# Fused RWKV, soft tree, attention and expert layers on one core: group-long runs of value matmuls, two head groups in one PSUM bank, single full-width transposes

## The chip, the cores and the metric

The kernel runs on one core of a Trainium2 chip. The time is the device time of one execution in microseconds (us). A core has a matrix engine (PE), which multiplies a stationary block of up to 128x128 by a moving block and adds into PSUM, and three other compute engines: VectorE (DVE), ScalarE (ACT) and GpSimd (POOL). PSUM has eight banks of 128 partitions by 512 floats. SyncE (SP) issues every DMA of this kernel, in one queue, in order. Each engine executes its own instructions in the order of the program and waits at an instruction until what it needs is there.

## The reference, cut to what matters

The input is 16 sequences of 512 positions with 128 features. Four sublayers follow one another, each followed by a layer normalisation of input plus output: an RWKV block (time mixing with two scans over the positions, then channel mixing), a soft decision tree of depth 8, causal attention, and a mixture of 16 experts of which two count at each position. The change touches the attention and the experts:

```python
scores = jnp.einsum('bthd,bshd->bhts', q, k) / jnp.sqrt(jnp.float32(dh))   # 16 heads of 8
scores = scores + causal[None, None, :, :]
weights = jax.nn.softmax(scores, axis=-1)
out = jnp.einsum('bhts,bshd->bthd', weights, v).reshape(b, seq, d)
...
topk_vals, topk_idx = jax.lax.top_k(s, TOP_K)
g_topk = jnp.sum(jax.nn.one_hot(topk_idx, N_r) * topk_vals[..., None], axis=-2)
routed = jnp.einsum('bse,bseo->bso', g_topk, xe)
```

## The kernel before

One sequence b is one batch of work; its 512 positions are four tiles of 128 (`NT`). The 16 heads are taken in four groups of four (`NG`, `HG`). Float32 operands of the queries and keys are split into three bfloat16 parts each, so that one bfloat16 matmul with 72 rows gives a score; three more rows of the query operand (`qo[QK_ROWS...]`) carry the negated row maximum, again in three parts, against a constant in the key operand.

For every batch and group of heads, these pieces follow one another:

- `operands` (line 833) loads the query and key operands of a group by DMA into one of three sets.
- `greatest` (line 854) computes the scores `sc` with queries on the partitions, adds the causal mask by one more matmul (stationary `identb`, moving `masks`, line 869), and DVE takes the maximum (line 871). POOL splits the 16 maxima of each partition into three bfloat16 parts (`nm3`, lines 876 to 881). PE turns the parts by four transposes of 128x12 into a bank `pmx`, one for each tile of positions (line 885), ACT copies 12x512 to `rows` (line 888), and three DMAs put the three parts into the query operand (line 891).
- `weighted` (line 910) computes the scores again with keys on the partitions, now with the maximum subtracted (`st`, line 927; mask at line 929), and ACT writes the exponentials into a tile `ew` of 128x4x512, one for each of the four key tiles kt. There are two such tiles (`e_slots`).
- `sums` (line 940) multiplies the exponentials by the values. The stationary operand has 32 columns: eight values of a head, a column of ones that gives the sum of the weights, and columns that are not used. Each of the four heads j writes its own 32 partitions of bank `o`, so a key tile is four float32 matmuls that run side by side (line 950). A key tile's four matmuls stand in PE's order as soon as its exponentials are due, so other PE work may lie between key tiles.
- `ends` (line 956) copies `o` to SBUF (`os`), turns it by four transposes (`pot`, line 969), and DVE divides by the sums (`rec`, `att`). After four groups come the output projection, the residual and the normalisation to `u`.
- `gating` (line 1007) finds the two greatest gates of each position, writes them into `gaug` (four tiles of 16 columns), turns them by four transposes (`pg`, line 1057), copies 16x512 to `gT` and sends it to DRAM with one DMA (line 1066), from where the gates are spread to all partitions (line 1080). `by_gate` multiplies `u` by each gate on POOL, `experts` sums the 16 experts in bank `acc`.

Ahead of these, `front` (line 570) computes the RWKV block and the tree of a batch.

All these pieces are Python generators that a planner (`Plan`, line 69) interleaves while the program is built: it keeps an estimated clock for each engine, with estimated costs (`tensor_us` and its like), and emits the instruction whose due time comes first, where the due time is the moment it became ready plus a slack by piece and engine (`S_FRONT` to `S_EXPERTS`). `PERIOD` and `LEAD` say when a batch's `front` may begin, `SCORES` how many banks may hold scores at a time. The planner fixes each engine's order; on the chip nothing is reordered by it. It sees the DMAs only as fixed delays, for instance 3.0 us for the rows of maxima.

Of the kernel before, what the change touches and what calls it, by code (L numbers as in the profile page):

```python
# [39 lines left out]

HAND_OVER = 0.2
BANKS = 8
SCORES = 5
PERIOD = 96.0

S_FRONT = {"PE": -6.0, "V": -6.0, "A": 0.0, "G": 0.0}
S_RWKV = {"PE": -10.0, "V": 3.0, "A": -30.0, "G": 3.0}
S_GREATEST = {"PE": -30.0, "V": 0.0, "A": -3.0, "G": 0.0}
S_WEIGHTED = {"PE": -15.0, "A": 3.0, "G": -10.0}
S_SUMS = {"PE": 10.0}  # L50
S_ENDS = {"PE": 6.0, "V": -3.0, "A": 0.0, "G": -15.0}
S_GATE = {"PE": 6.0, "V": 6.0, "A": 6.0, "G": 30.0}
S_EXPERTS = {"PE": 30.0}
FREE = {}
LEAD = 60.0
RWKV_PACE = 8.0
HOLD = 16
HOLD2 = 0
SPLIT = 2
EXPERT_PACE = 1.0  # L60
# [186 lines left out]
def tensor_us(op, out, w, x, *_):  # L247
    n = columns(out)
    if out.shape[0] == 32:
        return 0.02 + 0.0005 * n  # L250
    if x.dtype == BF16:
        return 0.02 + 0.0004 * n
    return 0.01 + 0.0009 * n if op == "transpose" else max(0.2, 0.0018 * n)
# [11 lines left out]
def pool_us(op, out, *_):  # L265
    return 0.25 + 0.0022 * columns(out)
# [3 lines left out]
def rwkv_tree_attn_moe(ctx: ExitStack, tc: tile.TileContext, a: dict, out: bass.AP):  # L270
# [30 lines left out]
    e_slots, us_slots, gb_slots = Slots(plan, 2), Slots(plan, 3), Slots(plan, 2)  # L301
# [28 lines left out]
    w_at = load("w_at", pool=p2, tag="e4")  # L330
# [108 lines left out]
    masks, idents = (fixed(x, [128, HG, 128], BF16) for x in ("masks", "idents"))  # L439
    mask, identb = masks[:, 0, :], idents[:, 0, :]  # L440
    w_qkv, w_o = fixed("w_qkv", [128, 3, D]), fixed("w_o", [128, D])

    vaug = fixed("vaug", [128, NT, NH * (DH + 1) + 23])
    vheads = vaug[:, :, 0:NH * (DH + 1)].rearrange("p t (h c) -> p t h c", c=DH + 1)
    qops, kops = ([fixed(f"{x}{i}", [128, HG, T], BF16) for i in range(OPERANDS)] for x in ("qop", "kop"))
    zeros = dram.tile([PARTS, HG, T], BF16, tag="zeros", name="zeros")

    def prepare_attention():

        G.memset(vaug, 1.0)  # L450
        for i in range(OPERANDS):
            for op, x in ((qops[i], 0.0), (kops[i], TWO_ONES)):
                V.memset(op.rearrange("p h t -> p (h t)").bitcast(F32), x)
            if i == 0:
                nc.sync.dma_start(out=zeros, in_=qops[i][0:PARTS])
            yield
# [4 lines left out]
        for i in range(HG):  # L461
            copy(masks[:, i, :], mask32)
            copy(idents[:, i, :], ident)
# [3 lines left out]
        for i in range(2):  # L467
            V.tensor_scalar(w_qkv[:, i, :].rearrange("p (d h) -> p d h", h=NH),
                            w_at[:, 2 * i * D:(2 * i + 1) * D].rearrange("p (h d) -> p d h", d=DH), col(V_NORM), None, ALU.mult)
            yield  # L470
# [8 lines left out]
    gaugs = [fixed(f"gaug{i}", [128, NT, NE]) for i in range(2)]  # L479
# [374 lines left out]
    def greatest():  # L854

        for b in range(B):
            for g in range(NG):
# [3 lines left out]
                for t in range(NT):  # L861
                    w = (t + 1) * 128
                    per = min(HG, 512 // w)
                    for h in range(0, HG, per):
# [4 lines left out]
                        mm(sc[:, :, t * 128:w], identb, masks[:, 0:per, :], start=False, stop=True)  # L869
# [6 lines left out]
                nm3 = p2.tile([128, NT, PARTS, HG], BF16, tag="nm3", name="nm3")  # L876
                yield
                G.tensor_copy(nm3[:, :, 0, :], nmx)
                G.tensor_tensor(nmx, nmx, nm3[:, :, 0, :], ALU.subtract)
                G.tensor_copy(nm3[:, :, 1, :], nmx)  # L880
                G.tensor_tensor(nm3[:, :, 2, :], nmx, nm3[:, :, 1, :], ALU.subtract)
                yield
                pt = yield from bank("pmx", (128, 512), BF16)
                for t in range(NT):
                    tr(pt[0:PARTS * HG, t * 128:(t + 1) * 128], nm3[:, t].rearrange("p a h -> p (a h)"), identb)
                yield
                rows = p2.tile([PARTS * HG, T], BF16, tag="rows", name="rows")
                copy(rows, pt[0:PARTS * HG, :])
                give(pt)
                for i in range(PARTS):  # L890
                    nc.sync.dma_start(out=qo[QK_ROWS + i:QK_ROWS + i + 1, :, :], in_=rows[HG * i:HG * (i + 1), :])
# [7 lines left out]
    def values(b, keep):  # L899
        if b:  # L900
            yield event("o", b - 1, NG - 1)
# [4 lines left out]
        copy(vheads[:, :, :, 0:DH], pv.rearrange("p (t h d) -> p t h d", t=NT, d=DH))  # L906
# [3 lines left out]
    def weighted():  # L910

        for b in range(B):
            for g in range(NG):
# [4 lines left out]
                for kt in range(NT):  # L918
                    slot_e = yield e_slots
                    n_q = T - kt * 128  # L920
                    per = min(HG, 512 // n_q)
                    e = p2.tile([128, HG, T], F32, tag="e4", name="ew")
                    for h in range(0, HG, per):
                        slot = yield scores
                        sc = yield from bank("st", (128, per, n_q))
                        for i in range(per):
                            mm(sc[:, i, :], ko[:, h + i, kt * 128:(kt + 1) * 128], qo[:, h + i, kt * 128:T],
                               start=(i == 0), stop=False)
                        mm(sc[:, :, 0:128], mask, idents[:, 0:per, :], start=False, stop=True)
                        yield  # L930
                        act(e[:, h:h + per, 0:n_q], sc, AF.Exp)
# [4 lines left out]
                    kept["e", b, g, kt] = e, slot_e  # L936
                    event("e", b, g, kt).set()
                sets.put(n)

    def sums():  # L940
        for b in range(B):
            yield event("values", b)
            for g in range(NG):
                for kt in range(NT):
                    yield event("e", b, g, kt)
                    e, slot_e = kept.pop(("e", b, g, kt))
                    if kt == 0:
                        o = yield from bank("o")
# [254 lines left out]
```

## Time and profile before

| What | Value |
|---|---|
| time of three runs | 1764.74, 1766.97 and 1767.44 us; median 1766.97 |
| span of the profiled execution, first to last instruction | 1762.0 us |
| granted PE clock, mean over the span | 0.970 |
| PE busy | 1623.4 us, 92% |
| DVE, ACT and POOL busy | 1270.0, 1172.3 and 1014.9 us |
| DMA | 133.78 MB, 24% of 16 engines' span |

The profile gives the span of its execution and no other time of it; the three times are those of runs of the same program, and their median is 5.0 us above the span.

Nearly all instructions are issued by one helper, so they carry one line number (L231), and groups are told apart by the names of their tiles: `o<-ew,vaug` is the matmul that writes bank `o` from the exponentials and the values. A float32 matmul appears as two records (x2 for one). "128*32" ahead of the shape is the part of the array that the stationary operand fills: 128 rows by 32 columns. In the timeline, the first number is the start in us from the span's beginning. Matmuls overlap: the duration of a record is the time from its start until its last result, while the time that it takes from PE is the distance from its start to the start of the next.

### The profile page before, as it was taken

How to read it: one execution, taken by the hardware profiler on the slowest of the kernel's cores; microseconds unless marked ns; L12 is line 12 of the kernel's file. 1: busy time of each engine (PE TensorE's matmuls, PEld its weight loads, DVE VectorE, ACT ScalarE, POOL GpSimd, SP SyncE). 2: the span in 40 equal slices, each digit the busy share in tenths (PEclk: the TensorE clock that was granted, in tenths of full speed). 3: DMA queues.
4: the chain of work that ended last, by engine and by line, in shares of the span. 5: the costliest groups of instructions: out<-in, count | busy, mean ns of one | idle time of the engine just before them, and what ended most of it. 6: DMA issues, size and time to landing. Idle time of an engine off the chain costs nothing.

```text
span 1762.0 us, 25378 instructions
## 1 busy us (share of the span) xinstructions
PE 1623.4 (92%) x8604; PEld 770.6 (44%) x8604; DVE 1270.0 (72%) x1928; ACT 1172.3 (67%) x1976; POOL 1014.9 (58%) x1321
## 2 busy tenths in 40 slices
PE   4567889899999999999999999999999999998976
PEld 1233334344444444454454444444444444454532
DVE  6686879687876869687776868687776868653633
ACT  3345677667768677777868677776768686675531
POOL 1345545557484756758474767757575746746323
PEclk8788999999999999999999999999999999999998
DMA  3001011212213232312222232312313122324323
GB/s 108 0 7 59 21 33 35 95 47 93 76 65 96 75 106 65 90 58 82 88 77 89 82 96 75 112 59 76 93 53 120 63 80 69 101 77 117 103 76 122
DMA packets 61970, 133.78 MB, mean 76 GB/s; under 512 B 11708, under 2 KB 32974, under 8 KB 61585
## 3 DMA queue, kind: packets, MB, share of 16 engines
q1 hardware_dynamic: 61841, 132.16, 24.1%
q8 instruction: 69, 1.13, 0.3%
q14 instruction: 60, 0.49, 0.1%
HBM read 114.01 MB, written 17.31 MB: 75 GB/s over the span
## 4 chain that ended last, share of the span: by engine, by line
PE 63%; DVE 11%; POOL 9%; ACT 6%; DMA 6%; issue 3%; SPq 1%; POOLq 0%; DVEq 0%; ACTq 0%
PE acc L231 9%; PE st L231 8%; PE sc L231 8%; PE p L231 7%; PE o L231 7%; PE pv L231 4%; DVE sk L231 4%; PE ph L231 3%; PE pr L231 3%; PE pk L231 2%; POOL us L231 2%; DMA gb<-gd 2%; DVE skv L231 2%; PE pvv L231 2%; POOL four L231 2%
## 5 line engine op out<-in xcount | busy, mean ns | idle before, releaser
L231 DVE TENSOR_REDUCE nmx<-sc 128x1 f32<-128x384 f32 (+3 forms) x704 | 439.0, 636 | 210.7 <-PE sc L231 208.8
L231 ACT ACTIVATE ew<-st 128x512 f32<-128x512 f32 (+1 forms) x704 | 380.8, 556 | 215.7 <-PE st L231 212.0
L231 POOL TENSOR_TENSOR us<-u,gb 128x512 f32<-128x512 f32 x240 | 306.5, 1287 | 186.5 <-PE acc L231 84.0
L231 PE MATMUL acc<-us,w_mo 128*128 128x512 f32 x512 | 268.8, 620 | 13.6 <-POOL us L231 11.5
L231 PE MATMUL st<-qop,kop 128*128 128x512 bf16 (+3 forms) x1024 | 254.5, 303 | 18.2 <-DMA qop<-rows 15.8
L231 PE MATMUL sc<-kop,qop 128*128 128x128 bf16 (+3 forms) x1024 | 256.6, 303 | 0.3
L231 DVE RECIPROCAL sk<-sk 128x512 f32<-128x512 f32 x64 | 213.9, 3343 | 0.0
L231 PE MATMUL o<-ew,vaug 128*32 128x512 f32 (+3 forms) x2048 | 191.5, 447 | 2.5 <-ACT ew L231 2.5
L231 PEld LDWEIGHTS <-qop 128*128 128x128 bf16 x1024 | 93.7, 99 | 183.2 <-issue 163.5
L231 PE MATMUL sc<-masks,idents 128*128 128x128 bf16 (+2 forms) x704 | 172.9, 246 | 0.0
L231 PE MATMUL st<-idents,masks 128*128 128x128 bf16 (+2 forms) x704 | 172.6, 245 | 0.0
L231 PEld LDWEIGHTS <-kop 128*128 128x128 bf16 x1024 | 91.1, 98 | 155.8 <-issue 109.5
L231 POOL TENSOR_TENSOR sk<-fk,sk 128x512 f32<-128x512 f32 x64 | 81.3, 1271 | 103.5 <-DVE sk L231 57.8
L231 POOL TENSOR_TENSOR skv<-t,skv 128x512 f32<-128x512 f32 x64 | 81.3, 1270 | 81.8 <-DVE skv L231 78.7
L231 POOL TENSOR_TENSOR lp<-gates,lp 128x8 f32<-128x8 f32 (+6 forms) x224 | 117.3, 545 | 2.3
L231 PEld LDWEIGHTS acc<-us,w_mo 128*128 128x128 f32 x512 | 83.0, 192 | 73.5 <-issue 39.0
L231 POOL TENSOR_TENSOR rw<-skv,sk 128x512 f32<-128x512 f32 x64 | 86.8, 1356 | 42.8 <-DVE sk L231 41.5
L231 PEld LDWEIGHTS <-idents 128*128 128x128 bf16 x704 | 69.4, 99 | 86.6 <-issue 80.8
L231 PE MATMUL pv<-sq,mean_w 128*128 128x512 f32 x160 | 91.0, 652 | 13.9 <-ACT sq L231 13.8
L231 DVE TENSOR_TENSOR_SCAN sk<-decay,k 128x511 f32<-128x511 f32 x64 | 102.8, 1606 | 0.0
L231 PE MATMUL p<-rw,w_tm 128*128 128x512 f32 x128 | 73.5, 658 | 29.8 <-POOL rw L231 25.6
L231 ACT ACTIVATE r<-pv,eps 128x512 f32<-128x512 f32 x96 | 65.8, 686 | 44.0 <-PE pv L231 25.9
(208 smaller groups left out, 2982.7 us busy)
## 6 DMA issues: line engine op xcount, KB each, us to landing
gb<-gd SPq DMA_DIRECT2D x128, 512.0 KB
qop<-there SPq DMA_DIRECT2D x576, 32.0 KB
kop<-there SPq DMA_DIRECT2D x192, 96.0 KB
there<-parts SPq DMA_DIRECT2D x32, 384.0 KB
x<-xT SPq DMA_DIRECT2D x16, 256.0 KB
out<-sqb SPq DMA_DIRECT2D x16, 256.0 KB
qop<-rows SPq DMA_DIRECT2D x192, 4.0 KB
w_mo<-w_mo SPq DMA_DIRECT2D x1, 1160.0 KB
```

The source lines that it names most:

```text
L231: ins = getattr(self.engine, op)(out, *args, **kw)
```

## The change

- `weighted` computes the key tiles in two pairs, (0, 3) and (1, 2). A pair's exponentials lie side by side in one tile of 128x4x640, of which there are three.
- `sums` waits for both pairs of a group and then issues all sixteen matmuls of the group in one run.
- Two groups share a bank `o`. In the values' layout a head now has 18 columns: nine zeros, eight values, a one. The even group of a pair of groups takes its 32 columns from the values on, the odd one from the zeros on, so their results fall into columns 0 to 8 and 9 to 17 of each head's 32 partitions, and one accumulates on top of the other. `ends` copies and turns a bank once for two groups. The columns of the query and key projections are permuted so that the heads come out in that order.
- The maxima's parts lie 32 columns apart by tile of positions in a fixed tile of 128x128, which one transpose turns; ACT copies 128x128. Four DMAs (one for each tile of positions, three rows by four heads by 128 positions) take the place of three. The gates are laid out, turned and sent likewise, with four DMAs for one.
- The causal mask and the identity are held once and repeated by a zero stride in the operand, not by four copies in memory.
- The planner's constants (slacks, `PERIOD`, `LEAD`, `SCORES`, costs) have other values.

```diff
+E_SLOTS = 3
+PAIRS = ((0, 3), (1, 2))
+HEAD = 2 * (DH + 1)
-SCORES = 5
-PERIOD = 96.0
+SCORES = 7
+PERIOD = 89.5
-S_FRONT = {"PE": -6.0, "V": -6.0, "A": 0.0, "G": 0.0}
...
+S_FRONT = {"PE": -6.0, "V": -21.0, "A": 0.0, "G": 1.0}
+S_RWKV = {"PE": -10.0, "V": 3.0, "A": -6.0, "G": 7.0}
+S_GREATEST = {"PE": -42.0, "V": -3.0, "A": -3.0, "G": 24.0}
+S_WEIGHTED = {"PE": -21.0, "A": 3.0, "G": -22.0}
+S_SUMS = {"PE": 1.0}
...
-LEAD = 60.0
+LEAD = 87.0
...
-                        mm(sc[:, :, t * 128:w], identb, masks[:, 0:per, :], start=False, stop=True)
+                        mm(sc[:, :, t * 128:w], identb, of_heads(mask, per), start=False, stop=True)
...
-                pt = yield from bank("pmx", (128, 512), BF16)
+                pt = yield from bank("pmx", (128, 128), BF16)
+                tr(pt, nm3.rearrange("p t c -> p (t c)"), identb)
+                yield
+                rows = p2.tile([128, 128], BF16, tag="rows", name="rows")
+                copy(rows, pt)
+                give(pt)
                 for t in range(NT):
-                    tr(pt[0:PARTS * HG, t * 128:(t + 1) * 128], nm3[:, t].rearrange("p a h -> p (a h)"), identb)
...
-                for i in range(PARTS):
-                    nc.sync.dma_start(out=qo[QK_ROWS + i:QK_ROWS + i + 1, :, :], in_=rows[HG * i:HG * (i + 1), :])
+                    nc.sync.dma_start(out=qo[QK_ROWS:QK_ROWS + PARTS, :, t * 128:(t + 1) * 128], in_=rows[32 * t:32 * t + PARTS * HG, :])
...
             for g in range(NG):
+                for i in range(2):
+                    yield event("e", b, g, i)
+                if g % 2 == 0:
+                    o = yield from bank("o")
                 for kt in range(NT):
-                    yield event("e", b, g, kt)
-                    e, slot_e = kept.pop(("e", b, g, kt))
-                    if kt == 0:
-                        o = yield from bank("o")
+                    e = kept.pop(("e", b, g, kt))
                     for j in range(HG):
-                        mm(o[32 * j:32 * (j + 1), kt * 128:T], vaug[:, kt, (HG * g + j) * (DH + 1):(HG * g + j) * (DH + 1) + 32], e[:, j, 0:T - kt * 128],
-                           start=(kt == 0), stop=(kt == NT - 1))
-                    e_slots.put(slot_e)
-                kept["o", b, g] = o
-                event("o", b, g).set()
+                        at = HEAD * (8 * (g // 2) + 2 * j + g % 2) + (DH + 1) * (1 - g % 2)
+                        mm(o[32 * j:32 * (j + 1), kt * 128:T], vaug[:, kt, at:at + 32], e[:, j, :],
+                           start=(g % 2 == 0 and kt == 0), stop=(g % 2 == 1 and kt == NT - 1))
+                for i in range(2):
+                    e_slots.put(kept.pop(("slot", b, g, i)))
+                if g % 2:
+                    kept["o", b, g // 2] = o
+                    event("o", b, g // 2).set()
+                yield
...
-            for t in range(NT):
-                tr(pg[0:NE, t * 128:(t + 1) * 128], gaug[:, t, :], ident)
+            tr(pg[:, 0:128], gaug.rearrange("p t c -> p (t c)"), ident)
...
-            nc.sync.dma_start(out=gd, in_=gT)
+            for t in range(NT):
+                nc.sync.dma_start(out=gd[:, t * 128:(t + 1) * 128], in_=gT[32 * t:32 * t + NE, :])
```

## The prediction

> **What bounds the kernel now.** I read the busy shares first, then the slices.
>
> ```profile
> PE 1623.4 (92%) x8604; PEld 770.6 (44%) x8604; DVE 1270.0 (72%) x1928; ACT 1172.3 (67%) x1976; POOL 1014.9 (58%) x1321
> ...
> PE   4567889899999999999999999999999999998976
> ...
> PEclk8788999999999999999999999999999999999998
> ```
>
> PE is at 90% or more in nearly every slice after the first seven, at full clock. Then the stretches of the middle (first number after the bounds: length, second: PE busy, then PEld, DVE, ACT, POOL):
>
> ```profile
> 400.00:600.00 200.00, 196.62 (x1078) 94.35 (x1077) 157.03 (x233) 146.17 (x248) 130.06 (x169) 1.00 0.26 81
> 800.00:1000.00 200.00, 198.73 (x1110) 95.14 (x1103) 154.82 (x231) 150.74 (x253) 129.84 (x163) 1.00 0.26 82
> 1200.00:1400.00 200.00, 197.12 (x1067) 94.25 (x1065) 152.26 (x227) 145.74 (x244) 133.29 (x175) 1.00 0.26 82
> ```
>
> PE is idle 1 to 2% there, the next engine (DVE) is busy 77%. So PE time taken out of this stage comes off the span, as long as PE still finds its inputs ready. A busy PE is not PE at its peak, so I read what each piece takes from start to start in the timeline of PE (start in us, duration, then the operation):
>
> ```profile
> 1270.59 1.02 PE L231 MATMUL pvv<-xv,w_tm 128*128 128x512 f32 x2
> 1271.44 1.02 PE L231 MATMUL p<-rw,w_tm 128*128 128x512 f32 x2
> 1272.39 1.71 PE L231 MATMUL o<-ew,vaug 128*32 128x512 f32 x16
> 1274.04 0.39 PE L231 MATMUL st<-qop,kop 128*128 128x256 bf16 x2
> ...
> 1275.56 1.02 PE L231 MATMUL acc<-us,w_mo 128*128 128x512 f32 x2
> 1276.52 0.39 PE L231 MATMUL pmx<-idents,nm 128*12 128x128 bf16 x4
> 1276.84 0.40 PE L231 MATMUL st<-qop,kop 128*128 128x128 bf16 x4
> 1277.07 0.38 PE L231 MATMUL st<-idents,masks 128*128 128x512 bf16 x1
> 1277.29 0.39 PE L231 MATMUL sc<-kop,qop 128*128 128x128 bf16 x4
> 1277.51 0.38 PE L231 MATMUL sc<-masks,idents 128*128 128x512 bf16 x1
> 1277.82 0.86 PE L231 MATMUL o<-ew,vaug 128*32 128x256 f32 x16
> 1278.61 1.13 PE L231 MATMUL acc<-us,w_mo 128*128 128x512 f32 x2
> 1279.57 0.60 PE L231 MATMUL pot<-ident,os 128*128 128x128 f32 x4
> 1280.01 0.38 PE L231 MATMUL sc<-kop,qop 128*128 128x256 bf16 x2
> ```
>
> The reader sees five prices. A float32 matmul of 512 columns takes 0.85 (1270.59 to 1271.44), but 0.95 when an `o` run follows, and the 512-column mask matmul takes 0.22 (1277.07 to 1277.29), but 0.31 ahead of `o`: entering the 32-column form costs 0.09 to 0.10. The run of 512 and 384 columns takes 1.65; four heads side by side should take 0.85 + 0.64 (384/512 of it) = 1.49, so leaving costs about 0.10 and the staggered starts the rest. In all a run costs 0.19 on top of its columns, whether it holds one key tile or two. A float32 matmul that follows such a run takes 0.96, another 0.10. `pmx` pays the same toll: 0.10 ahead of it, then 0.32 for four transposes. A float32 transpose takes 0.11 (four in 0.44).
>
> **The change part by part, against the span of 1762.0.** Run lengths are counted in the order of the two built programs.
>
> 1. Value matmuls. Before, 210 runs of four and 23 of eight, 233 in all; after, 64 of sixteen. Columns are the same. 169 runs less at 0.19: -32.1.
> 2. Maxima. 64 times 0.10 + 0.32 goes, 64 times 0.056 comes (a 128-column bfloat16 matmul at full width, from the median start-to-start distance of the mask matmuls): -23.3.
> 3. `pot`: 32 banks less to turn, 4 x 0.11 each: -14.1. `pg`: 48 transposes less: -5.3.
> 4. Float32 matmuls behind a narrow run: 86 after `o` and 28 after `pmx` before, 6 after `o` in the changed order. 108 x 0.10 = -10.8. But 44 now stand behind a full-width `pmx`; a 512-column float32 matmul behind such a short one takes 0.055 more (median first pass 485 ns against 429): +2.4.
>
> PE's own work falls by 83.1, about 5.2 of some 96 per batch. The head gains nothing from it: the order up to the first scores is nearly the same (108 instructions against 111), and PE is idle a third of that time.
>
> 5. Off PE, hidden under its 98%: ACT loses 32 copies of `os` (0.577) and half of each `rows` copy (0.566 to about 0.29, the 128x128 cast's time) and `gT` copy, and gains 4 table loads at 1.28: about -36 of 1172. DVE has 32 `rec` and `att` pairs less but of twice the size, about -10. If PE were no longer the cover these would be gains too.
> 6. SP: 64 + 48 more DMAs. One `qop<-rows` takes 0.578 to issue, one `gd<-gT` 0.315: at most 52 on a queue that mostly waits. Queued behind them are operand loads and gate spreads (`gb`), issued well ahead. What matters is the rows' landing: before, the shortest way from the last `pmx` to the first `st` is 0.26 + 0.57 copy + 1.83 issue + 1.2 = 3.9; after, 0.26 + 0.29 + four issues + 1.2, that is 2.9 (at 0.29 an issue, as operand loads have) to 4.2 (at 0.6). I take 4.2, the row of the same small transfer. PE's work between the two in the order (priced by the start-to-start distances above) has a median of 6.3 before and 5.4 after; groups where it is shorter than the chain miss 9.0 in sum before and 13.4 after. PE waited 15.8 for these rows before. So +4, between -5 and +12.
> 7. PE work between the last `sc` and `pmx` falls from a median of 4.2 to 3.1, while the chain under it (a 0.68 reduction, four POOL steps of 0.22) is about 2.5: shortfall 3.5 before, 7.0 after, +4, between 0 and +8.
> 8. The new wait: a run of sixteen waits for the whole group's exponentials, and all PE work stands behind it. PE work between a group's last `st` and its last value matmuls: median 3.7 before, 2.8 after. One exponential takes 0.595. If ACT is some 2 us behind, the shortfall over 64 groups goes from 8.0 to 18.3; at 4.2 (a backlog of the seven banks that `SCORES` allows) from 65.7 to 107.1. Before, PE waited 2.5 there and its loads 10.0, which sits near the 2 us reading: +5, between -2 and +41.
> 9. The end: work after the last value run falls from 35.9 to 32.2 because four of batch 14's experts move ahead of it: -3; the four `gd` issues add 0.95 there and the shorter copy takes 0.3 off, inside it.
> 10. Mask by zero stride: I take 0, since columns set PE's time. If repeated columns were read at half rate, the forms with two or four repeats (256 x 0.109 + 128 x 0.216) would cost +55; no row shows a gain.
>
> **Rules against rows.** The Trainium skill, "TensorEngine Tiling (Array Packing)", Key Properties, says that changing the tiling mode drains the array, and gives no price. With the fixed 166 ns of a warm matmul's latency from "TensorE: Matmul & The Clock Gate", Single matmul latency, as an estimate of one drain, two per run would make term 1 -56, 24 us better. The trace shows 0.09 and 0.10, and the sum goes by the trace.
> Against the change speaks "DMA: Bandwidth & Descriptors", whose quick table wants at least 512 B per piece; the rows now go in pieces of 256 B. The same page says that SBUF to SBUF is spared. No run here shows a 256 B piece; by the table the landing would be later than in term 6 by an amount that it does not give.
>
> **Sum.** 1762.0 - 83.1 + 4 + 4 + 5 - 3 = 1689 for the span. The median of the runs stands 5.0 above the profiled span, so 1694.
>
> **Rivals.**
> - A, the covers give way in part. Terms 6, 7 and 8 at their upper ends (12 + 8 + 41 = 61 in place of 13): 1742. For it: the cover is thinner at all three places. Against: waits of PE on these inputs were small before, although some groups had too little cover then too.
>
> ```profile
> PE st L231 <- DMA qop<-rows: 15.8, 12, 4.2
> ...
> PE pmx L231 <- POOL nm L231: 13.5, 10, 4.8
> ...
> PE o L231 <- ACT ew L231: 2.5, 3, 1.0
> ```
>
> - B, slower: ACT becomes what the group's run waits for. It turns the sign when each group waits 1.3 more (83 / 64), so when ACT is on average 2.8 + 1.3 = 4.1 behind at the run. If it lags a group's whole set of exponentials (11 x 0.55 = 6.0), the 64 runs wait 3.2 each: 1694 - 5 + 205 = 1894. For it: one block behind eleven exponentials, seven score banks. Against: ACT is busy 73% of the middle and loses work; `ew` runs as the planner costs it (0.6).
> - C, slower: zero-stride operands are slow in every mask matmul (these take 113 in all): 1694 + 113 = 1807; with the repeated ones alone 1749.
> - D, no effect: PE's busy time is filler, and something slower sets the pace. DVE, next, has 79 of 110 us per batch, and the page's chain of work lies on PE for 63% of the span against 11% on DVE. It would give 1767.
>
> **How the numbers follow.** The forecast (1666 to 1720) 0.70, A (1720 to 1755) 0.17, B 0.07, C 0.03, D 0.03. Low end: no new waits (13 off) and a planner order that closes part of the 30 us PE idles after 1600: 1666. High end: the larger part of A, 1738, which leaves out about 0.2. What a measurement can tell from no change is 0.2%, 3.5 us. Faster: the forecast, A and a little of C, 0.88; same 0.02 (of D); slower 0.10 (B, the rest of C and D).
>
> **What would show it.** Right: `o` records in runs of 32 (two for each matmul) that take about 2.3 from their start to the next matmul (0.85 + 0.64 + 0.43 + 0.21 of columns, and the staggered starts and exit), `pmx` as single records with no 0.10 ahead of them, the batch period of PE down from about 96 to 91, PE still 97% or more in 400 to 1400. Wrong: PE waiting tens of us for `ew`, `nm` or rows; mask matmuls of two or four repeats above 0.109 and 0.216 apart; ACT or SP ending PE's idle time each group.

## The result: 0.9% slower, and the profile after

The changed kernel takes 1780.8 us (median of four runs, 1779.1 to 1782.8) against 1766.1 before. The ratio is 1.009, with a 95% interval of 1.007 to 1.010. The forecast was 1694. The profiled execution's span went from 1762.0 to 1779.7.

The page after, its lines of busy time, slices and chain:

```profile
PE 1570.6 (88%) x8236; PEld 775.7 (44%) x8236; DVE 1255.6 (71%) x1866; ACT 1135.7 (64%) x1942; POOL 1016.6 (57%) x1326
...
PE   5667798898999989898998989899999999999975
...
PEclk9777899999999999999999999999999999999998
...
PE 56%; POOL 14%; DVE 11%; DMA 7%; ACT 5%; issue 4%; SPq 2%; POOLq 0%; DVEq 0%; ACTq 0%
```

PE is 53 us less busy, and 8s now stand among the 9s of its middle slices. POOL holds 14% of the chain that ended last; before it was 9%. The same three stretches as before:

```profile
400.00:600.00 200.00, 183.48 (x999) 90.84 (x998) 142.74 (x214) 137.06 (x234) 126.18 (x158) 0.98 0.28 84
800.00:1000.00 200.00, 186.46 (x1005) 92.57 (x1004) 144.61 (x215) 137.25 (x235) 127.27 (x166) 0.97 0.25 79
1200.00:1400.00 200.00, 190.83 (x1060) 97.44 (x1058) 154.03 (x226) 143.29 (x250) 127.30 (x165) 0.99 0.26 81
```

PE was busy 197 to 199 of each 200 us and is now busy 183 to 191, and the granted clock, 1.00 before, is 0.97 to 0.99. What each piece takes on PE can be read from the timeline of PE after:

```profile
1002.26 0.27 PE L236 MATMUL st<-identb,mask 128*128 128x256 bf16 x1
1002.37 1.02 PE L236 MATMUL acc<-us,w_mo 128*128 128x512 f32 x2
...
1006.90 2.36 PE L236 MATMUL o<-ew,vaug 128*32 128x512 f32 x32
1009.19 0.39 PE L236 MATMUL sc<-kop,qop 128*128 128x512 bf16 x1
...
711.65 0.22 PE L236 MATMUL pmx<-identb,nm 128*128 128x128 bf16 x1
711.71 1.08 PE L236 MATMUL acc<-us,w_mo 128*128 128x512 f32 x2
```

A group's sixteen value matmuls come as one run of 32 records and take 2.29 (1006.90 to 1009.19). `pmx` takes 0.06, and a mask matmul of 256 repeated columns 0.11. All of this is as forecast. To compare whole kernels I price every matmul by the start-to-start distance of its kind (the shortest fifth of each kind of neighbouring pair, over all traces) and call the rest of the time waiting, which includes slower clock. So priced, PE's work fell from 1551 to 1468, by 83, the forecast's own number. Its waiting rose from 203 to 304, and nearly all of that in one place: between 400 and 1600 us from 32 to 130. In the rest of this text "waiting in the middle" means this measure. It depends on what counts as one kind: with the pairs grouped by shape, by name or by whole runs, the same traces give 67 to 77 for the fall in work and 87 to 94 for the rise in the middle. A count without prices agrees with the 98. These are the sums of six stretches of 200 us from 400 to 1600, before and after:

```profile
sum 1200.00, PE 1183.24 PEld 568.45 DVE 904.24 ACT 875.14 POOL 775.00; mean PE 197.21 PEld 94.74 DVE 150.71 ACT 145.86 POOL 129.17
```

```profile
sum 1200.00, PE 1114.80 PEld 556.26 DVE 876.96 ACT 823.70 POOL 759.49; mean PE 185.80 PEld 92.71 DVE 146.16 ACT 137.28 POOL 126.58
```

PE is idle 68 us more, and half clock (below) loses up to 29, together 97. The question is where those 98 us come from. PE's waits after, from the view of waits:

```profile
PE p L236 <- POOL rw L236: 41.6, 11, 9.3
PE st L236 <- DMA qop<-rows: 39.5, 28, 5.5
PE pmx L236 <- POOL nm L236: 29.2, 25, 3.6
PE acc L236 <- POOL us L236: 24.6, 10, 5.2
PE pv L236 <- ACT sq L236: 13.7, 15, 1.8
...
PE sc L236 <- DMA qop<-rows: 6.5, 3, 2.7
```

Before, the first four stood at 25.6, 15.8, 13.5 and 11.5. The prediction shows two of these lines; the other two are:

```profile
PE p L231 <- POOL rw L231: 25.6, 7, 8.6
...
PE acc L231 <- POOL us L231: 11.5, 7, 4.3
```

All four grew, and three of the four come from POOL. No wait of `o` for `ew` is in the list: the group-long run does not stall.

Waits also cost twice. In the timeline of PE around 951 us:

```profile
945.72 0.60 PE L236 MATMUL pout<-ident,rb 128*128 128x128 f32 x4
951.04 2.07 PE L236 MATMUL acc<-us,w_mo 128*128 128x512 f32 x2 [4.72 <-POOL us L236]
952.91 0.52 PE L236 MATMUL st<-qop,kop 128*128 128x384 bf16 x1
```

and in windows around it (the third column from the right is the granted clock):

```profile
943.00:950.40 7.40, 3.00 (x19) 1.55 (x17) 4.42 (x7) 4.37 (x9) 1.68 (x3) 1.00 0.86 251
950.40:957.20 6.80, 6.16 (x15) 2.66 (x16) 1.01 (x2) 3.08 (x5) 5.47 (x5) 0.50 0.42 133
957.20:964.00 6.80, 6.80 (x19) 2.99 (x19) 3.04 (x5) 5.42 (x10) 2.19 (x6) 1.00 0.45 147
```

PE waits 4.72 for a gated product and then runs at half clock for 6.8 us; the `acc` matmul takes 1.87 from start to start in place of 0.86. Between 400 and 1600 the trace has 58 us of such stretches, 14 of them, 3.4 or 6.8 long each. Before, it has none there. Work at half clock takes twice as long, so up to 29 of the 98 us are this.

### The profile page after: what moved, and what is told of

Same layout as the page of the kernel before. It is cut to its first block, busy times and chain, and to the rows that moved or that the text cites. A ratio compares the mean times of both kernels' runs of the same rounds, so it can differ in the third digit from the quotient of the medians.

```text
span 1779.7 us, 24755 instructions
## 1 busy us (share of the span) xinstructions
PE 1570.6 (88%) x8236; PEld 775.7 (44%) x8236; DVE 1255.6 (71%) x1866; ACT 1135.7 (64%) x1942; POOL 1016.6 (57%) x1326
## 4 chain that ended last, share of the span: by engine, by line
PE 56%; POOL 14%; DVE 11%; DMA 7%; ACT 5%; issue 4%; SPq 2%; POOLq 0%; DVEq 0%; ACTq 0%
PE acc L236 8%; PE st L236 8%; PE sc L236 8%; PE p L236 7%; PE o L236 6%; PE pv L236 4%; DVE sk L236 4%; DMA gb<-gd 3%; POOL four L236 3%; POOL us L236 3%; PE pr L236 3%; DMA qop<-rows 3%; PE ph L236 2%; PE pvv L236 2%; PE pk L236 2%
## 5 line engine op out<-in xcount | busy, mean ns | idle before, releaser
L236 PE MATMUL acc<-us,w_mo 128*128 128x512 f32 x512 | 273.4, 625 | 24.9 <-POOL us L236 24.6
L236 PE MATMUL st<-qop,kop 128*128 128x512 bf16 (+3 forms) x1024 | 254.7, 305 | 45.4 <-DMA qop<-rows 39.5
L236 PE MATMUL sc<-mask,identb 128*128 128x128 bf16 (+2 forms) x704 | 174.7, 248 | 0.0
L236 PE MATMUL st<-identb,mask 128*128 128x128 bf16 (+2 forms) x704 | 173.8, 247 | 0.0
L236 PE MATMUL o<-ew,vaug 128*32 128x512 f32 (+3 forms) x2048 | 156.4, 447 | 0.0
L236 POOL CAST nm<-nmx 128x16 bf16<-128x16 f32 x128 | 26.2, 205 | 142.7 <-DVE nmx L236 138.6
L236 PEld LDWEIGHTS o<-ew,vaug 128*32 128x32 f32 x2048 | 61.5, 112 | 105.5 <-issue 86.3
L236 PEld LDWEIGHTS <-identb 128*128 128x128 bf16 x704 | 70.1, 100 | 84.8 <-issue 77.9
```

The costliest lines, as they stand in the source:

```text
L236: ins = getattr(self.engine, op)(out, *args, **kw)
```

## Experiments

Theories on trial, with the letters that the expectations use. P: the planner's new constants. R: the rows of maxima land later. S: the long run of value matmuls holds PE up. F: the order of before happens to fit the chip's delays, and neighbouring orders do not. L: other engines' queues and latencies nearly set the pace, so PE time taken out becomes waiting. W: PE sets the pace and single new waits are added to it.

### Constants and the order

**Old constants on the new dataflow:** all slacks, `PERIOD`, `LEAD`, `SCORES`, paces and costs, of which one line is shown.

```diff
-S_GREATEST = {"PE": -42.0, "V": -3.0, "A": -3.0, "G": 24.0}
+S_GREATEST = {"PE": -30.0, "V": 0.0, "A": -3.0, "G": 0.0}
...
```

> The changed kernel with all planner constants and cost estimates of the kernel before; its dataflow is untouched. Theory P (the planner's new constants give an order whose covers are too thin): 1685 to 1715, since PE's work is about 90 us less and the waits of PE in 400 to 1600 go back to some 30 us. Theory R (the landing of the maxima's rows is what grew: four DMAs take 3.0 to issue where three took 1.83): PE still waits about 40 for the rows, the rest falls: 1740 to 1770. Theory S (the run of sixteen blocks PE): 1775 or more.

It took 1811.6 us, and the ratio to before is 1.025 (1.021 to 1.028). PE waits 77 us for rows alone. The time lies in the range given for S, but PE does not wait for exponentials ahead of `o` here either, so it is no evidence for S.

**New constants on the old dataflow**, the same lines the other way round.

> The kernel before with the changed kernel's planner constants and cost estimates. Theory P: the new waits and half-clock stretches appear here too, 1820 to 1870 (some 100 us on 1766). Theory R and theory S: 1750 to 1785, no half-clock stretches in 400 to 1600.

It took 1826.8 us, 1.034 (1.031 to 1.036), as P has it: the new constants cost the old dataflow 60 us. But the old constants do not mend the new dataflow, so P as the whole cause falls. The run with the nudged order below shows that part of both numbers can be the luck of an order.

**The planner told the rows' longer way.**

```diff
-                plan.go(plan.end + 3.0, landed(b, g))
+                plan.go(plan.end + 4.4, landed(b, g))
```

> The changed kernel with the planner told 4.4 us from the end of the rows' copy to their landing (measured: 3.04 issue and 1.2), not 3.0. Theory R: the planner puts other work in between, waits for rows fall below 15: 1725 to 1755. Theory P: the order changes without the other waits going away: 1765 to 1795.

It took 1783.8 us, 1.010 (1.007 to 1.013), the second reading. The wait of `st` for rows fell from 39.5 to 27.3, but waiting in the middle is 126 against 130. The order is a new one here.

**A nudge of the order of before.**

```diff
-S_SUMS = {"PE": 10.0}
+S_SUMS = {"PE": 9.0}
```

> The kernel before with one slack changed by one (S_SUMS 10 to 9): the same instructions in another order. Theory F (the order before is one that fits, and orders next to it do not): 1780 to 1815 with PE's waits in 400 to 1600 two to three times as long. If orders near it are as good: 1760 to 1772.

It took 1791.0 us, 1.014 (1.011 to 1.016). One unit in one slack costs more than the whole change did. Waiting in the middle doubles, 32 to 61, and 24 us of half clock appear. So F has something to it: an order's luck is worth as much as the result that is to be explained, and only kernels of one order can be compared finely. The experiments on single inputs below therefore keep the order of PE, DVE, ACT and POOL to the instruction.

### Is PE the pace?

**PE work taken out, order kept,** on the changed kernel and on the one before:

```diff
-                        mm(sc[:, :, 0:128], mask, of_heads(identb, per), start=False, stop=True)
+                        plan.did("PE", tensor_us("matmul", sc[:, :, 0:128], mask, mask))
```

> The changed kernel in its own order, without the 704 mask matmuls on the transposed scores (the causal mask is left out there), which take 57 us of PE from start to start; the planner still charges for them, so nothing else moves. Theory L (in this order something other than PE sets the pace, so PE time taken out turns into waits): 1755 to 1780, less than half of the 57 comes off. Theory W (PE sets the pace and the waits are added on top): 1720 to 1735.

> The kernel before, likewise without the 704 mask matmuls and otherwise in its own order. Theory L (even the order before only just covers the other engines' delays): 1735 to 1766, less than half of the 57 comes off. Theory W: 1705 to 1720.

704 matmuls worth 57 us leave PE. After: 1754.5 us, 26 less. Before: 1733.4 us, 34 less. Both times lie 0.5 to 2 us outside L's ranges and 13 to 20 from W's, so this speaks for L with a larger share than it named: 0.46 of PE's time comes off the span after and about 0.6 before, and the rest turns into waiting (in the middle 130 to 151 after, 32 to 64 before). PE was 98% busy before, but its inputs were only just in time.

### The rows of maxima

**The old way of the maxima** (four transposes, 12x512 copy, three DMAs) in the changed kernel:

```diff
-                tr(pt, nm3.rearrange("p t c -> p (t c)"), identb)
+                for t in range(NT):
+                    tr(pt[0:PARTS * HG, t * 128:(t + 1) * 128], nm3[:, t, 0:PARTS * HG], identb)
...
-                for t in range(NT):
-                    nc.sync.dma_start(out=qo[QK_ROWS:QK_ROWS + PARTS, :, t * 128:(t + 1) * 128], in_=rows[32 * t:32 * t + PARTS * HG, :])
+                for i in range(PARTS):
+                    nc.sync.dma_start(out=qo[QK_ROWS + i:QK_ROWS + i + 1, :, :], in_=rows[HG * i:HG * (i + 1), :])
```

> The changed kernel with the maxima's way as before: four transposes of 128x12, a copy of 12x512 and three DMAs (the row tile has one buffer for want of room). PE's work rises by about 23. Theory R: PE's waits for the rows fall from 46 to about 16 and the half-clock stretches go with them: 1720 to 1755. Theory P: 1785 to 1805.

It took 1803.2 us, 1.020 (1.018 to 1.023), in the range given for P. The wait of `st` for rows fell to 21.9, PE's work rose by 18, and waiting in the middle stayed at 131. The planner drew a new order here, so this run says little about R.

**No row DMAs at all,** order kept:

```diff
-                for t in range(NT):
-                    nc.sync.dma_start(out=qo[QK_ROWS:QK_ROWS + PARTS, :, t * 128:(t + 1) * 128], in_=rows[32 * t:32 * t + PARTS * HG, :])
```

> The changed kernel in its own order, without the 256 DMAs of the maxima's rows: the scores are not shifted by their maxima (that part of the computation is left out), and nothing waits for the rows. Theory R (the rows' landing is the cause): PE's 46 us of waits for rows go and most of the 58 us of half clock in 400 to 1600 with them, 1690 to 1715. Theory F (the order as a whole does not fit the chip's delays, and the rows are one place of many): 1735 to 1760, the other waits stay or grow.

It took 1746.0 us, 0.988 (0.985 to 0.990), 35 us less. That bounds R at 35 us, where its own range asked for 66 or more, and lies in F's range: the rows are one place of several, and the waits for `rw`, `nm` and `us` stay at 41.9, 27.8 and 28.1. Why the rows land later shows in the view of the tile `rows`, in the DMA lines (shortest, median and longest issue in ns), before and after:

```profile
L891 SPq DMA_DIRECT2D qop<-rows x192: 572/578/708, 192.4 to 1693.6; - x192
```

```profile
L903 SPq DMA_DIRECT2D qop<-rows x256: 697/703/873, 187.1 to 1714.5; - x128
```

An issue of three rows by four heads takes 0.70, not 0.58, and there are four.

**One row DMA,** order kept: the parts lie in the first 48 of the 128 columns, by part, head and tile.

```diff
-                first_part, second, third = (nm3[:, :, HG * i:HG * (i + 1)] for i in range(PARTS))
+                first_part, second, third = (nm3.rearrange("p t c -> p (t c)")[:, NT * HG * i:NT * HG * (i + 1)].rearrange("p (h t) -> p t h", t=NT) for i in range(PARTS))
...
-                for t in range(NT):
-                    nc.sync.dma_start(out=qo[QK_ROWS:QK_ROWS + PARTS, :, t * 128:(t + 1) * 128], in_=rows[32 * t:32 * t + PARTS * HG, :])
+                nc.sync.dma_start(out=qo[QK_ROWS:QK_ROWS + PARTS, :, :], in_=rows[0:PARTS * HG * NT, :])
```

> The changed kernel with one DMA per group in place of four for the rows of maxima: the maxima's parts lie in the first 48 of the 128 columns, ordered by part, head and tile of positions, so that 48 partitions of 128 positions go to the three rows of the query operand in one issue. Nothing else differs, and the order on PE, DVE, ACT and POOL is the changed kernel's. From the traces: the row chain takes 0.26 + 0.25 + 2.97 (four issues) + 1.2; with one issue of 0.70 about 2.3 us of it goes. Leaving the DMAs out altogether gave -35 us. Theory R (the rows' landing is the main new wait) expects most of that back, -20 to -35 us, a median of 1746 to 1761, which would be under the kernel before; waits of st and sc for rows from 46 to below 10. Theory L/F (PE's waits move to the next input whichever one is mended; the order happens to fit or not) expects 0 to -15, with the waits for nm, rw or us going up as those for rows go down.

It took 1756.8 us, 0.993 (0.991 to 0.995), 24 us less, and faster than before. Its waits:

```profile
PE p L236 <- POOL rw L236: 40.9, 11, 7.4
PE acc L236 <- POOL us L236: 28.6, 13, 5.4
PE pmx L236 <- POOL nm L236: 25.3, 22, 3.7
```

The rows are gone from the top of the list; POOL's outputs stay about where they were. For this input R's reading holds, and L's does not: the price stood by itself.

**The same on the kernel before** (one DMA in place of three):

> The kernel before with one DMA per group in place of three for the rows of maxima (twelve partitions of 512 positions to three rows in one issue); the order on PE, DVE, ACT and POOL is the one before. Three issues of 0.578 become one, about 1.1 us less in a row chain of 3.9. PE waited 15.8 for these rows. If the rows cost the same here as in the changed kernel, in proportion to the waits (15.8 against 46), -7 to -12 us: about 1757. If the order before already covers its rows, within 5 us of the kernel before.

It took 1758.1 us, 0.995 (0.994 to 0.997), 9 us less, in proportion to its smaller wait.

### POOL's products and the maxima's parts

**Shorter gated products,** order kept (the planner still charges 512 columns), on the changed kernel, and then together with the one row DMA:

```diff
-                us = p3.tile([128, T], F32, tag="us", name="us")
-                (W if b >= B - SPLIT and q % 2 else G).tensor_tensor(us, kept[b]["u"], gb[:, q % 2, :], ALU.mult)
+                us = p3.tile([128, 128], F32, tag="us", name="us")
+                (W if b >= B - SPLIT and q % 2 else G).tensor_tensor(us, kept[b]["u"][:, 0:128], gb[:, q % 2, 0:128], ALU.mult)
...
-                mm(acc, w_exp[:, q, :], us, start=False, stop=(q == NE - 1))
+                mm(acc, w_exp[:, q, :], of_heads(us, NT), start=False, stop=(q == NE - 1))
```

> The changed kernel with the products of the normalised input and the gates computed for 128 of the 512 positions; the experts' matmuls read those 128 columns four times over, so they take the same time and the other positions' gated values are left out. The planner charges the full cost, so the order on every engine is the changed kernel's. 240 products on POOL at 1.294 us become about 0.45: some 200 us of POOL's 1017 go. PE waited 41.6 for rw, 29.2 for nm and 24.6 for us, all from POOL. A theory that POOL's queue is what PE's new waits come from expects half of these 95 or more to go: -45 us or better, about 1735. Theory R (rows) expects at most -10. Theory L (waits move to the next input) expects -5 to -25, and waits for rows or others going up.

> The changed kernel with both edits: one DMA per group for the rows of maxima, and the products of the normalised input and the gates computed for 128 of 512 positions (the other positions' gated values are left out). The order on PE, DVE, ACT and POOL is the changed kernel's. Each edit alone took about 24 us off. With the rows mended, the waits for rows fell to about 4 and those for POOL's outputs stayed (rw 41, us 29, nm 25); with POOL shortened, the waits for rows stayed at 36 and rw, us and nm fell to 33, 18 and 24. If each late input has its own price, the two add up: 1781 - 24 - 25 = about 1732 (1726 to 1738), with PE's waits between 400 and 1600 at about 90. If waits only move to the next late input, the second edit brings less on top of the first: 1742 to 1757, with the remaining waits on DVE and ACT outputs up. If POOL's waits behind the row DMAs were what held it, more than the sum: under 1726.

Alone it took 1755.8 us, 0.994 (0.992 to 0.995), 25 less; a product takes 0.485 in place of 1.294, and the waits for `rw`, `us` and `nm` only fall to 33, 18 and 24. That is the edge of L's range, and little more than half of what the theory of POOL's queue asks. Together they took 1716.2 us, 0.971 (0.969 to 0.973), 65 less, which is more than 24 + 25. A reading that fits is that two late inputs hide each other: where both are late, mending one shows only part of it. Waits do not simply move on to the next input here, as L has it.

**Both on the kernel before:**

> The kernel before with both edits: one DMA per group for the rows of maxima, and the products of the normalised input and the gates computed for 128 of 512 positions (the other positions' gated values are left out); the order on PE, DVE, ACT and POOL is the one before. The same two edits took 65 off the changed kernel, down to 1716. If the late inputs swallowed the gain, they have little to give here, since PE waits only 33 us between 400 and 1600: from 1758 (row DMA alone) to 1748 to 1757, so that the change is worth 30 to 40 us where the inputs are early. If the two edits are worth the same in any order of the work, 1700 to 1710, and the change brings nothing even with early inputs, so that something else sets the pace.

It took 1745.1 us, 0.988 (0.984 to 0.991), only 21 less. With these inputs early in both, the change is worth 29 us (1745 to 1716).

**A third input made early:** the transpose reads the parts of the group before.

```diff
-                tr(pt, nm3.rearrange("p t c -> p (t c)"), identb)
+                tr(pt, nm3s[(g + 1) % 2].rearrange("p t c -> p (t c)"), identb)
```

> The changed kernel with both edits (one DMA for the rows, gated products for 128 of 512 positions) and a third: the full-width transpose of the maxima's parts reads the tile of the group before, which is long there, in place of the group's own. The scores are so shifted by another group's maxima; POOL still computes all the parts. The order on PE, DVE, ACT and POOL is the changed kernel's. PE waited 20.6 for these parts (16 times) and 1716 was the time. If each late input has its own price, 1716 less 15 to 25: 1691 to 1701, and with the kernel before given the same at about 1740, the change is worth over 40. If the waits move on to the next inputs (rw, us, sq, scores), 1706 to 1716.

> The kernel before with both edits and the third: the four transposes of the maxima's parts read the tile of the group before, which is long there (the scores are shifted by another group's maxima). The order on PE, DVE, ACT and POOL is the one before. PE waited 8.3 for these parts (5 times) and 1745 was the time. If each late input has its own price, 1737 to 1742; if the waits move on, 1742 to 1748.

After, it took 1706.0 us, 0.966 (0.965 to 0.968), 10 less than with two. Before, it took 1744.9, no less than with two. Both are in the range for waits that move on. The change is now worth 39.

### The gates' DMA

**One gate DMA on top of one row DMA,** order of the four compute engines kept, nothing left out:

```diff
-            gate = gaug[:, :, 0:NE]
+            gate = gaug.rearrange("p t c -> p (t c)")[:, 0:NT * NE].rearrange("p (e t) -> p t e", t=NT)
...
-            for t in range(NT):
-                nc.sync.dma_start(out=gd[:, t * 128:(t + 1) * 128], in_=gT[32 * t:32 * t + NE, :])
+            nc.sync.dma_start(out=gd.rearrange("e (t n) -> (e t) n", t=NT), in_=gT[0:NT * NE, :])
```

> The changed kernel with one DMA for the rows of maxima and also one for the gates (the gates' columns lie in the first 64 of 128, ordered by expert and tile of positions, so that 64 partitions go to DRAM in one issue). The order on PE, DVE, ACT and POOL is the changed kernel's; nothing is left out. Four issues at 0.43 become one, some 1.1 to 1.3 us earlier landing once per batch. With the rows' DMA alone the time was 1757 and PE waited 28.6 for the gated products. If SP's queue makes these late, 16 batches at up to 1.2 us: 5 to 19 us off, 1738 to 1752, and that wait falls by 10 or more. If the spread waits for the operand store that stands in SP's order in between, or the cover is there in most batches, within 5 us of 1757.

It took 1725.4 us, 0.976 (0.974 to 0.977), 31 us less than with the row DMA alone, more than either reading allowed, and the fastest complete kernel of the study, 2.4% under the kernel before. Of its waits:

```profile
PE p L236 <- POOL rw L236: 40.9, 11, 7.4
PE pmx L236 <- POOL nm L236: 28.0, 23, 3.7
...
PE acc L236 <- POOL us L236: 9.9, 8, 4.4
```

The wait for gated products fell from 28.6 to 9.9. SP's timeline shows what came earlier, in the changed kernel ahead of the wait at 951:

```profile
934.82 2.97 SPq L903 DMA_DIRECT2D qop<-rows  x4
937.97 1.71 SPq L1088 DMA_DIRECT2D gd<-gT  x4
943.03 0.39 SPq L839 DMA_DIRECT2D there<-parts  x1
943.61 1.98 SPq L1102 DMA_DIRECT2D gb<-gd  x2
```

and the same batch with one issue each:

```profile
917.49 0.73 SPq L902 DMA_DIRECT2D qop<-rows  x1
920.72 0.51 SPq L1086 DMA_DIRECT2D gd<-gT  x1
922.61 0.81 SPq L1100 DMA_DIRECT2D gb<-gd  x2
925.79 0.90 SPq L839 DMA_DIRECT2D there<-parts  x2
```

In the changed kernel the next batch's operand store stands ahead of the gate spread `gb` on SP, the store waits until 943.03 for `parts` from POOL, and the spread waits behind it: 5.6 us from the gates' first issue to the spread's, against 1.9. Summed over the sixteen batches that distance is 43.1 before, 71.6 after, 71.0 with the row DMA mended and 44.2 with both. SP's order is not the planner's (it knows DMAs as delays only), and it came out different with the edit.

**Is it that order?** With one row DMA and four gate DMAs, each rows' DMA is held behind the gate spread written ahead of it:

```diff
+                with tc.issue_after(spreads[-1].ins) if spreads else nullcontext():
+                    nc.sync.dma_start(out=qo[QK_ROWS:QK_ROWS + PARTS, :, :], in_=rows[0:PARTS * HG * NT, :])
...
+                spreads.append(nc.sync.dma_start(out=gb, in_=gd[2 * q:2 * q + 2].partition_broadcast(128)))
```

> The changed kernel with one DMA for the rows of maxima and four for the gates as it has them, and each rows' DMA held behind the gate spread that was written ahead of it, so that SP issues the first gate spreads before the rows' DMA, which waits for a transpose. Nothing is left out; the order on PE, DVE, ACT and POOL is the changed kernel's. With the one rows' DMA alone it was 1757 and PE waited 28.6 for gated products; with one gates' DMA too, 1725 and 9.9. If the order on SP is what made the gates late, 1725 to 1740 and that wait under 15. If the issue time of the four DMAs is, 1750 to 1760 and the wait stays near 28.

It took 1760.0 us, 0.995 (0.993 to 0.997): no gain, and the wait is still 27.5, which is the reading by issue time. The sum of distances fell only to 62.0: three batches in which the operand store, not the rows, stands ahead of the spread still have 5.6. Rows ahead of the spread are not the cause. The same batch here, on SP and on PE:

```profile
925.10 1.98 SPq L1091 DMA_DIRECT2D gd<-gT  x4
930.16 0.39 SPq L840 DMA_DIRECT2D there<-parts  x1
930.74 0.96 SPq L1105 DMA_DIRECT2D gb<-gd  x2
```

```profile
937.58 2.08 PE L237 MATMUL acc<-us,w_mo 128*128 128x512 f32 x2 [4.13 <-POOL us L237]
```

and with one issue each, on PE, without a wait:

```profile
928.91 1.02 PE L236 MATMUL acc<-us,w_mo 128*128 128x512 f32 x2
```

The traces say more than the times. PE's long waits for gated products between 400 and 1600 fall on just those three batches: 4.0, 4.3 and 5.0 with the row DMA alone, 4.1, 4.2 and 4.9 here, none with one gate DMA. Around the end of each, 3.4 or 6.8 us of half clock begin, and with one gate DMA there are none at these places. That is 13 us of waiting and 6 to 7 us lost by half clock, together some 20 of the 31. One issue in place of four brings the spread forward by about 1.0 where nothing stands between (2.9 to 1.9), and by 3.7 in these three batches, where the store also moves behind the spread. So most of the 31 lies with the store ahead of the spread, whose place changed as a side effect of the edit. No run moved the store alone; this division is read from traces, not shown by a run.

**All four edits:**

> The changed kernel with all four edits: one DMA for the rows, one DMA for the gates, gated products for 128 of 512 positions (the other positions' gated values are left out), and the transpose of the maxima's parts reading the tile of the group before (the scores are shifted by another group's maxima). The order on PE, DVE, ACT and POOL is the changed kernel's. Without the gates' edit it took 1706, and the kernel before with its three took 1745. If the gates' DMA has its own price of 31, about 1675, and the change is worth 70 of its 83 where all these inputs are early. If shorter products already leave the gates time, the edit brings 0 to 12: 1694 to 1706, and some 30 to 45 of the 83 stay lost to waits spread over the rest.

It took 1679.2 us, 0.950 (0.949 to 0.952), 27 below the run with three. Its waits begin:

```profile
PE p L236 <- POOL rw L236: 35.2, 10, 7.4
PE st L236 <- DMA qop<-rows: 18.1, 15, 3.8
PE pv L236 <- ACT sq L236: 17.6, 22, 2.6
```

Against the kernel before with the same inputs early (1744.9; its gates' DMA was one all along) that is 66 us less. Two of the four edits leave work out, so this measures the cause and is no kernel to be had. Half clock in the middle is down from 58 to 10 us, waiting there from 130 to 60.

## Why the prediction was wrong

**Right.** Terms 1 to 4: PE's work was to fall by 83.1, and fell by 83 as priced above (67 to 77 with other groupings); runs, `pmx` and repeated masks cost what their terms said, so rival C's slow zero strides do not exist here. Term 8 and rival B: the long run does not wait for exponentials (S falls); the forecast's +5 was nothing. Term 9: from the last value matmul to the end the kernel took 58.6 us before and 54.5 after, 4 less where the term said 3.

**Wrong: the first step, "PE time taken out of this stage comes off the span, as long as PE still finds its inputs ready".** The condition carried everything, and terms 6 to 8 filled it with three inputs and +13 us; the measured rise of the waiting is 98. What the runs put in its place, with the order held:

| Input that is made early | after | before |
|---|---|---|
| rows of maxima: four issues to one (before: three to one) | -24 | -9 |
| gates: four issues to one, with the new order on SP, on top | -31 | not needed |
| gated products shorter and maxima's parts early, on top | -46 | -13 |
| time then | 1679 | 1745 |

The prices depend on the sequence in which they are taken: the row DMA and the shorter products gave 24 and 25 alone, 65 together. Together they turn 15 us of loss into 66 us of gain: 81 of the 98.

**Term 6** failed twice. The rows' landing was priced at 0.6 an issue, and an issue took 0.70, so the shortest way of a group is 4.8 and not 4.2. PE's waits for rows rose by 30 (15.8 to 46.0 with those of `sc`), where the term gave +4 with a bound of +12; by the runs, one issue gives 24 back after and 9 before. The smaller pieces were not the reason: the shortest time from the end of the last issue to the first `st` is 1.18 before, with pieces of 1 KB, and 1.10 after, with 256 B. So what the Trainium skill ("DMA: Bandwidth & Descriptors", Specifications) asks for line rate, 512 B, did not matter for transfers of this size from SBUF to SBUF, which the same page spares, as the prediction says; the number of issues did. And it set the gates' four issues aside: "Queued behind them are operand loads and gate spreads (`gb`), issued well ahead". They were not: in three batches the spread stood behind a store that waited for POOL, and the edit of the gates gave 31 back. A queue that mostly waits is not a free queue, because what it waits for stands ahead of everything behind it.

**Term 7** put the cover of `pmx` at +4 up to +8; PE's wait for the maxima's parts rose by 16 (13.5 to 29.2). **Missing** from the sum were two more outputs of POOL that PE waits for, `rw` and `us` (+16 and +13; 13 to 14 us of the waits for `us` after are those behind the late spread), and half clock after waits, up to 29 of the 98 us and part of the prices above. The low end of the range hoped to close part of PE's idle time after 1600 us; waiting there went from 37 to 40.

**Rivals.** A had the mechanism, covers that give way, but counted three of them and stopped at 61; it could not lose. D came nearest, 1767, and had half of a reason: PE's time is not filler, but in the two runs that took 57 us out only 0.46 and 0.6 of it came off while the inputs were just in time.

**Open.** Some 17 of the 98 us: even with all four inputs early PE waits 60 us in the middle against 22. The largest of its waits is `rw`, 35.2 against 27.3 in the kernel before with its three, an input that no run made early by itself; why it grew is not shown. How much of the rest is the draw of the order (F) was not separated; the nudged kernel shows that this could be all of it.

## What to carry to other kernels

An engine that is 98% busy may be the pace and still not pay out what is taken from it: list every input that it waits for, with the slack of each, before the saving is booked, and hold the order fixed when testing them. One transfer cut into four costs the queue four issues, and what stands behind them can be a different stage's work: pack the layout so that one issue does it, and look at what the queue issues in which order. Here one issue in place of four at two places, and the order on SP that came with it, turned a 0.9% loss into a 2.4% gain.

## What the runs showed of the hardware

- The time of a DMA's issue on SP depends on its pattern: a gates' row block of 16 partitions 0.31 (16x512) and 0.42 in the median when it goes by tiles, 64 partitions at once 0.51; rows 0.58 for one row of the operand, 0.70 to 0.74 in the median for three, whether 12 or 48 partitions are sent. So one large issue costs about what one of its four parts did.
- Half clock comes in stretches of 3.4 or 6.8 us on a PE that is 93% busy in its stage (1115 of 1200 us); at 98 to 99% it had none in 1200 us. The Trainium skill ("TensorE: Matmul & The Clock Gate", HAM oscillation) gives the loss as half of the throttled time, and its rule is no idle gap over about 3.4 us. The stretch at 951 followed a gap of 4.72, as the rule has it; but another, at 636.4, followed gaps of at most 1.74, in windows of the changed kernel:

```profile
633.00:636.40 3.40, 1.37 (x6) 0.56 (x5) 2.77 (x7) 1.88 (x4) 2.25 (x2) 0.99 0.24 77
636.40:643.20 6.80, 5.61 (x14) 2.23 (x13) 1.44 (x2) 2.53 (x5) 4.95 (x8) 0.50 0.16 59
```

  There PE was busy 1.37 of 3.40 us. Here several short waits close together were followed by half clock as one long one was.
- One unit of slack in the planner moved the time by 1.4%, with the same work in another order.
